# Layer 0 of a four-layer network: PSUM pairs in a ring, both halves of the scores in a row, and the head mixing behind the product with v

## The chip, the cores and the metric

The kernel runs on one core of one Trainium2 chip. The metric is the device time of the whole program in microseconds, the median of several runs. One further execution was taken by the hardware profiler; its trace gives the start and duration of every instruction on each engine.

## The reference

The input is a tensor of 4 images of 512 channels by 32x32 positions. Four layers follow, each of the form x = x + f(gn(x)), where gn is a group normalization over 32 groups. The change touches layer 0 alone, which is an attention with mixed heads:

```python
q = einsum('oc,bct->bot', w_q, xf).reshape(b, heads, hd, t)     # k and v alike; 8 heads of 64, t = 1024
attn = einsum('bhdq,bhdT->bhqT', q, k) * scale
attn = einsum('gh,bhqT->bgqT', w_head, attn)                    # every output head mixes all input heads
attn = softmax(attn, axis=-1)
attn = (attn - mean) / sqrt(var + EPS) * gamma + beta           # one mean and variance per head and image
out = einsum('bhqT,bhdT->bhqd', attn, v)                        # then a projection, a bias, and x is added
```

Layers 1 (a channel gate from a small simulated circuit), 2 (an attention) and 3 (a lookup of eight rows of a memory) follow it.

## The kernel before, in words

Layer 0 treats the images one after another. For one image, q, k and v are projected, and then the 1024 queries are walked in 32 steps of 32 queries (`NS`, `STEPS`), each over all 8 heads and all 1024 keys. All products are in 32-bit floats. The work of a step, in the order in which data passes:

- `scores(b, s, n)` (lines 440 to 465), for the two halves n of the keys: 8 small matmuls of 64 rows (each recorded as two, x16 in the trace) into a pair of PSUM banks, called `sc`, and a copy of the pair by ScalarE into half of the SBUF tile `ss` (L457), of which there are two in turn. Behind the second half, eight DMAs of 128 KB, four issued on SP and four on GpSimd (POOL) in turn, bring the rows of `ss` into the tile `s2` with the heads beside each other (L464). `s2` has two buffers as well.
- `mix(b, s)` (L471), two steps later (`old = s - 2`): 32 small matmuls with the head weights from `s2` into two more pairs of PSUM banks, `mx0` and `mx1`.
- `exps` (L478): ScalarE's exponential of each pair into half of the single tile `e`.
- `turn_keys` (L484): VectorE (DVE) transposes each half of `e` into `eT`, which holds a block of four steps and has two buffers.
- `reduce` (L500): eight `bn_stats` on DVE give the sums and squares of `e`.
- `sums(b, j)` (lines 519 to 570), once for a block of four steps, as a generator that is moved on by `next`: POOL adds up (L532), PE sums over partitions into the bank `pt` (L535), DVE takes the reciprocal out of `pt` (L538), and POOL spreads it by DMA and adds to the sum of squares.
- `apply(b, s - LAG)` (L511): 32 matmuls of `eT` with v into the bank `pv`, `LAG = 6` steps behind the scores. After four of them `take_out` copies `pv` by ScalarE (L574), and `scale` multiplies on POOL and sends the block off.

[...] `pt` serves whatever is small: the projection of v in steps 0 to 6 (`take_v`, L410), the sums (L535), the sum of v in steps 7 and 8 (`sum_v`, L421 and L431), the group means of the next image in steps 25 and 27 (L150 and L160 in `group_coeffs_parts`), those of the previous image's gate from step 28 on, and in steps 12 to 27 of images 1 to 3 the output projection of the image before, a sixteenth in each step (`put_quarter`, L684). The functions `mid` and `piece` hand these out to the steps; `early` issues the loads, on ScalarE's queue, three of 256 KB in each of steps 7 to 10 (what the image before left) and 28 to 31 (the next image and its w_q).

The order is written out by hand. `pin` keeps an instruction behind everything already traced on its engine, so each engine works through its list in the order of the program, and waits at the first entry that is not ready. A tile's buffer is handed on only when the last reader of the old content is done. A step of before is, on PE: scores of half 0, mix of the step two back, scores of half 1, the sums (one step in four), `mid`, the product with v, `piece`. After the 32 steps, `LAG` more run the pipeline dry, with the next image's q projected in the first four; its k follows.

Of the kernel before, what the change touches and what calls it, by code (L numbers as in the profile page):

```python
# [16 lines left out]
P = 128  # L17
# [24 lines left out]
def fast_net(ctx: ExitStack, tc: tile.TileContext, a: dict, out: bass.AP, flag: bass.AP):  # L42
# [6 lines left out]
    stage = ctx.enter_context(ExitStack())  # L49
    ps_a = stage.enter_context(tc.tile_pool(name="ps_a", bufs=1, space=PSUM))  # L50

    pairs = {at: ps_a.tile([P, 2, NB], F32, tag=at, name=at) for at in ("sc", "mx0", "mx1")}
    pv_bank = ps_a.tile([P, NB], F32, tag="pv", name="pv")
    pt_bank = ps_a.tile([P, NB], F32, tag="pt", name="pt")

# [124 lines left out]

    def place(at, name):

        return pairs[at] if at else ps_s.tile([P, 2, NB], F32, tag="sc", name=name)

    def flat2(ps):
        return ps.rearrange("p n q -> p (n q)")

    def tokens(src):
        return lambda k, n: src[:, k, n * NB:(n + 1) * NB]
# [37 lines left out]


    STEPS = T // NS
    LAG = 6  # L230
    NK = T // 4
    apool = ctx.enter_context(tc.tile_pool(name="attn", bufs=1))
    img = [dict() for _ in range(B)]
# [51 lines left out]
    def put_q(q, m):  # L285
        return lambda ps: pin(nc.scalar.copy(q[:, m, :], ps))

    def first():

        I = img[0]  # L290
        xn = I["xn"] = big("xn", "xn_0")
        w = I["w_q"] = eight_k([P, KC, C], "w_q0_0", 0)
        for k in range(KC):
            nc.sync.dma_start(out=xn[:, k, :], in_=x_v[0, :, k, :])
            nc.sync.dma_start(out=w[:, k, :], in_=a["w_q"][:, k, :])
        I["w_k"] = load_w("w_k", "w_k0_0", 1)
# [12 lines left out]

        def means(k):  # L310
            next(parts[k])
            next(parts[k])

        def deviations(k):
            next(parts[k])
            found[k] = next(parts[k])

        def normalize(k):
            gm, rstd, dm = found[k]
            pin(nc.vector.tensor_scalar(  # L320
                xn[:, k, :], xn[:, k, :], gm, rstd, ALU.subtract, ALU.mult))
            pin(nc.gpsimd.tensor_mul(ybar[:, k:k + 1], dm, rstd))

        def multiply(k, m):
            for n in range(T // NB):
                pin(nc.tensor.matmul(
                    pairs[f"mx{m}"][:, n, :],
                    w[:, k, m * P:(m + 1) * P], xn[:, k, n * NB:(n + 1) * NB],
                    start=(k == 0), stop=(k == KC - 1),
                ))  # L330

        stats(0)
        means(0)
        stats(1)
        deviations(0)
        means(1)
        normalize(0)
        for k in range(KC):
            if k + 2 < KC:
                stats(k + 2)  # L340
            multiply(k, 0)
            if k + 1 < KC:
                deviations(k + 1)
            multiply(k, 1)
            if k + 1 < KC:
                normalize(k + 1)
            if k + 2 < KC:
                means(k + 2)
        for m in range(2):
            put_q(q, m)(flat2(pairs[f"mx{m}"]))  # L350
        for m, at in ((2, "sc"), (3, "mx0")):
            project(w, tokens(xn), m, at, put_q(q, m))

    def prepare(b):

# [84 lines left out]
    def scores(b, s, n):  # L440


        I = img[b]
        q, k_ = I["q"], I["k"]
        if n == 0:
            I["ss", s] = eight_k([P, 2, T], f"ss_{b}_{s}", s % 2)
        ss = I["ss", s]
        sc = pairs["sc"]
        for m in range(KC):
            for r in range(2):  # L450
                pin(nc.tensor.matmul(  # L451
                    sc[m * NS:(m + 1) * NS, r, :],
                    q[r * HD:(r + 1) * HD, m, s * NS:(s + 1) * NS],
                    k_[r * HD:(r + 1) * HD, m, n * NB:(n + 1) * NB],
                    start=True, stop=True,
                ))
        pin(nc.scalar.copy(ss[:, :, n * NB:(n + 1) * NB], sc))  # L457
        if n == 0:
            return
        s2 = I["s2", s] = apool.tile([P, 2, T], F32, tag="s2", bufs=2, name=f"s2_{b}_{s}")  # L460
        del I["ss", s]
        for m in range(KC):
            for r in range(2):
                pin(relays[r].dma_start(  # L464
                    out=s2[r * KC + m::NH], in_=ss[m * NS:(m + 1) * NS, r, :]))

    def mix(b, s):
        s2 = img[b].pop(("s2", s))
        for t in range(4):
            for r in range(4):  # L470
                pin(nc.tensor.matmul(  # L471
                    pairs[f"mx{r // 2}"][t * NS:(t + 1) * NS, r % 2, :].rearrange("p (qq k) -> p qq k", qq=2),
                    wmix[r * NS:(r + 1) * NS], s2[r * NS:(r + 1) * NS, :, t * NK:(t + 1) * NK],
                    start=True, stop=True,
                ))

    def exps(s, half):
        pin(nc.scalar.activation(  # L478
            e[:, half].rearrange("p r qq k -> p (r qq k)"), flat2(pairs[f"mx{half}"]), AF.Exp))

    def turn_keys(s, half):

# [4 lines left out]
            e[:, half].rearrange("p r qq (b x) -> p r qq b x", x=NS),  # L487
        ))

    def reduce(b, s):  # L490

        I = img[b]
        j, i = divmod(s, 4)
        if i == 0:
            I["st", j] = apool.tile([P, 4, 4, 2, 6], F32, tag="st", bufs=2, name=f"st_{b}_{j}")
        st = I["st", j]
        for half in range(2):
            for r in range(2):
                for qq in range(2):
                    pin(nc.vector.bn_stats(st[:, i, 2 * half + r, qq, :], e[:, half, r, qq, :]))  # L500

    def apply(b, s):

# [652 lines left out]

    first()
    circuit()
    for m, at in enumerate(("mx1", "sc", "mx0", "mx1")):
        take_k(0, m, at)  # L1160

    def step(b, s, mid, piece):


        I = img[b]
        old = s - 2
        j, part = divmod(s - LAG, 4)
        tiled = 0 <= j < TC
        if tiled and part == 0:
            I["tail"] = sums(b, j)  # L1170
            next(I["tail"])
        if s == 0:
            take_v(b, 0)
        if s < STEPS:
            scores(b, s, 0)
            early(b, s)
        if 0 <= old < STEPS:
            mix(b, old)
            exps(old, 0)
            turn_keys(old, 0)  # L1180
        elif s < STEPS:
            piece(b, s)
        if s < STEPS:
            scores(b, s, 1)
        if 0 <= old < STEPS:
            exps(old, 1)
        if tiled and part == 0:
            next(I["tail"])
        mid(b, s)
        if tiled:  # L1190
            apply(b, s - LAG)
            if part == 3:
                take_out(b, j)
        if 0 <= old < STEPS:
            turn_keys(old, 1)
            reduce(b, old)
        if old >= 0:
            piece(b, s)
        if tiled and part < 3:
            next(I["tail"], None)  # L1200
        if tiled and part < 2 and j > 0:
            next(I["scale"])
        if tiled and part == 3:
            I["scale"] = scale(b, j)
            next(I["scale"])
# [44 lines left out]
    for b in range(B):  # L1250
# [9 lines left out]
            nxt[keys[2]] = load_w(keys[2], f"{keys[2]}_n{b}", 1)  # L1260
        qs = chunks(take_q2, 0) if last else chunks(take_q, b + 1)
        ks = chunks(take_k2, 0) if last else chunks(take_k, b + 1)
        places = dict(zip(range(STEPS, STEPS + KC), ("sc", "sc", "mx0", "mx1")))
        for s in range(STEPS, STEPS + LAG):
            step(b, s, lambda b, s: next(state["behind"], None),
                 lambda b, s: qs[s - STEPS](places[s]) if s in places else None)
# [5 lines left out]
        for m, at in enumerate(("sc", "mx0", "mx1", "mx0")):  # L1272
            ks[m](at)
        if last:
            run_out(instance_norm(b))
            bv2 = apool.tile([P, C], F32, tag="o2", name="bv2")
            nc.sync.dma_start(out=bv2, in_=a["bv"].partition_broadcast(P))
            for i, at in enumerate(("mx0", "mx1", "sc", "mx0")):
                take_v2(0, i, at)
            for m, at in enumerate(("mx1", "sc", "mx0", "mx1")):  # L1280
                put_out(b, m, at)

    stage.close()
    pairs.clear()
# [796 lines left out]
```

## Time and profile before

| | us |
|---|---|
| median of 3 runs (2708.62 to 2716.2) | 2716.14 |
| the profiled execution's own time | 2713.05 |
| its span, first to last instruction | 2711.3 |
| PE busy, 95% of the span | 2578.0 |
| DVE busy, 55% | 1502.3 |
| POOL busy, 46% | 1236.3 |
| ScalarE (ACT) busy, 37% | 1007.6 |
| mean granted TensorE clock | 0.986 |

The first scores of layer 0 start at 75.1 us of the span and the last mixing at 1244.8; layer 0 is thus a little less than half of the program. In a row of a group of instructions stand the line, the engine, the operation, what it writes and reads, how often it ran, its busy time, the mean of one, and how long the engine stood idle just before it and for what. In a row of the timeline stand the start, the duration, the engine, the line and, in brackets, the idle time before it with its releaser.

### The profile page before, as it was taken

The page shows a single profiled execution, that of the slowest core. Times are in us where ns is not written, and L with a number is a line of the kernel's source. Part 1 is how long each engine was busy: PE and PEld are TensorE (multiplying, and loading weights), DVE is VectorE, ACT ScalarE, POOL GpSimd, SP SyncE. Part 2 cuts the span into 40 slices and gives each one's busy share as a digit, 9 for nine tenths or more (in the row PEclk, how much of TensorE's full clock was granted, in tenths as well). Part 3 has the DMA queues.
Part 4 walks back from the last instruction along what each step waited for, and adds up shares of the span by engine and source line. Part 5 has one row for each costly group of instructions (what it writes and reads, how often), then busy time and mean ns, then how long its engine had stood idle before and what let it go on. Part 6 is the DMA issues. An engine that isn't in the chain of part 4 may idle for free.

```text
span 2711.3 us, 46987 instructions
## 1 busy us (share of the span) xinstructions
PE 2578.0 (95%) x18286; PEld 1144.8 (42%) x18286; DVE 1502.3 (55%) x2386; ACT 1007.6 (37%) x1149; POOL 1236.3 (46%) x1891
## 2 busy tenths in 40 slices
PE   8988999989989899989999999999999999999995
PEld 3343534545345443545433443343344334444442
DVE  4487337871478516873146225414513437888887
ACT  1465336551565415652145025215403632121211
POOL 2266415552356514654057027305602725666665
PEclk9999999999999999999999999999999999999997
DMA  2487438880588627885410030022002016767665
GB/s 79 122 209 205 137 92 217 217 226 30 142 227 217 175 61 188 206 201 180 142 55 1 32 124 1 16 78 63 1 31 93 1 51 190 221 187 215 183 183 161
DMA packets 159320, 349.81 MB, mean 129 GB/s; under 512 B 32361, under 2 KB 65129, under 8 KB 155378
## 3 DMA queue, kind: packets, MB, share of 16 engines
q1 hardware_dynamic: 88352, 167.17, 21.5%
q0 software_dynamic: 49152, 142.79, 19.6%
q10 hardware_dynamic: 21586, 36.76, 4.7%
q8 instruction: 147, 2.41, 0.4%
q14 instruction: 83, 0.68, 0.1%
HBM read 178.57 MB, written 33.69 MB: 78 GB/s over the span
## 4 chain that ended last, share of the span: by engine, by line
PE 83%; DMA 6%; ACT 4%; DVE 3%; issue 2%; POOL 2%; SPq 1%; ACTq 0%; POOLq 0%; DVEq 0%
PE at L1094 16%; PE sc_c L973 8%; PE pv_c L1006 8%; PE mx L197 7%; PE sc L451 7%; PE pv L511 6%; DMA s<-ss 5%; PE p L197 4%; PE sc L197 4%; PE pt L410 4%; PE q L197 3%; PE v L209 3%; PE k L197 3%; PE pt L684 3%; ACT ss L457 3%; PE mx L471 2%
## 5 line engine op out<-in xcount | busy, mean ns | idle before, releaser
L484 DVE STREAM_TRANSPOSE eT<-e 128x1024 f32<-128x1024 f32 x256 | 317.4, 1242 | 269.5 <-ACT e L478 267.4
L464 POOL DMA_DIRECT2D s<-ss x512 | 259.3, 514 | 374.1 <-ACT ss L457 306.9
L1111 POOL DMA_INDIRECT got<-in_mem,ix x256 | 280.0, 1094 | 216.1 <-DVE tmx L1117 92.7
L457 ACT COPY ss<-sc 128x1024 f32<-128x1024 f32 x256 | 258.9, 1011 | 259.7 <-PE sc L451 201.5
L967 ACT ACTIVATE eT<-sc_c 128x1024 f32<-128x1024 f32 x256 | 247.8, 1022 | 278.5 <-PE sc_c L973 215.2
L500 DVE BATCH_NORM_STATS2 st<-e 128x6 f32<-128x256 f32 x1024 | 341.5, 405 | 0.0
L991 POOL TENSOR_TENSOR e<-eT 128x1024 f32<-128x1024 f32 x96 | 230.5, 2403 | 176.7 <-ACT eT L967 145.9
L451 PE MATMUL sc<-k,q 64*32 64x512 f32 x4096 | 285.3, 613 | 21.1 <-ACT ss L457 16.2
L478 ACT ACTIVATE e<-mx 128x1024 f32<-128x1024 f32 x256 | 262.5, 1029 | 62.2 <-PE mx L471 31.6
L992 DVE TENSOR_TENSOR eT<-eT,e 128x1024 f32<-128x1024 f32 x96 | 131.5, 1370 | 249.0 <-POOL e L991 248.8
L511 PE MATMUL pv<-eT,v 128*64 128x128 f32 x4096 | 254.8, 278 | 0.0
L511 PEld LDWEIGHTS pv<-eT,v 128*64 128x64 f32 x4096 | 224.5, 138 | 61.6 <-issue 60.0
L973 PE MATMUL sc_c<-q,k 64*128 64x512 f32 x1024 | 238.6, 605 | 2.3 <-DVE xr L650 2.3
L987 POOL TENSOR_TENSOR eT<-eT 128x1024 f32<-128x1024 f32 x32 | 81.1, 2534 | 348.5 <-ACT eT L967 336.9
L1006 PE MATMUL pv_c<-eT,v 128*64 128x512 f32 x1024 | 232.2, 596 | 0.0
L471 PE MATMUL mx<-s,wmix 32*32 32x512 f32 x4096 | 158.9, 621 | 48.3 <-DMA s<-ss 45.3
L1135 DVE SCALAR_TENSOR_TENSOR acc<-got,et,acc 128x512 f32<-128x512 f32 x224 | 168.5, 752 | 8.0
L1033 DVE RECIPROCAL ri_c<-ri_c 128x512 f32<-128x512 f32 x32 | 107.1, 3345 | 96.1 <-ACT ri_c L1032 96.1
L973 PEld LDWEIGHTS sc_c<-q,k 64*128 64x128 f32 x1024 | 94.2, 187 | 131.9 <-issue 73.6
L1099 ACT COPY att<-at 128x1024 f32<-128x1024 f32 x64 | 64.8, 1012 | 218.0 <-PE at L1094 217.9
L587 POOL TENSOR_TENSOR o<-pv,rb 64x256 f32<-64x256 f32 x128 | 111.0, 867 | 68.2 <-ACT pv L574 61.3
L1006 PEld LDWEIGHTS pv_c<-eT,v 128*64 128x64 f32 x1024 | 70.6, 137 | 152.6 <-issue 151.7
(316 smaller groups left out, 3236.0 us busy)
## 6 DMA issues: line engine op xcount, KB each, us to landing
s<-ss SPq DMA_DIRECT2D x512, 128.0 KB
s<-ss POOLq DMA_DIRECT2D x512, 128.0 KB, 4.5
rb<-r POOLq DMA_DIRECT2D x64, 128.0 KB, 6.1
o<-o SPq DMA_DIRECT2D x32, 256.0 KB
xr<-in_x ACTq DMA_DIRECT2D x32, 256.0 KB
x<-xr SPq DMA_DIRECT2D x32, 256.0 KB
xr_c<-x SPq DMA_DIRECT2D x32, 256.0 KB
x<-xr_c SPq DMA_DIRECT2D x32, 256.0 KB
```

What stands on the lines that cost most here:

```text
L197: pin(nc.tensor.matmul(ps[:, n, :], w[:, k, m * P:(m + 1) * P], rhs(k, n), start=(k == 0), stop=(k == KC - 1),))
L451: pin(nc.tensor.matmul(sc[m * NS:(m + 1) * NS, r, :], q[r * HD:(r + 1) * HD, m, s * NS:(s + 1) * NS], k_[r * HD:(r + 1) * HD, m, n * NB:(n ...
L457: pin(nc.scalar.copy(ss[:, :, n * NB:(n + 1) * NB], sc))
L464: pin(relays[r].dma_start(out=s2[r * KC + m::NH], in_=ss[m * NS:(m + 1) * NS, r, :]))
L478: pin(nc.scalar.activation(e[:, half].rearrange("p r qq k -> p (r qq k)"), flat2(pairs[f"mx{half}"]), AF.Exp))
L484: pin(nc.vector.transpose(eT[:, j % 2].rearrange("p b (qq i r) x -> p i r qq b x", qq=2, i=4)[:, i, 2 * half:2 * half + 2], e[:, half].rea ...
L500: pin(nc.vector.bn_stats(st[:, i, 2 * half + r, qq, :], e[:, half, r, qq, :]))
L511: pin(nc.tensor.matmul(pv[r * HD:(r + 1) * HD, gp, :], I["v"][:, t, g * HD:(g + 1) * HD], eT[:, j % 2, t, :, 4 * g:4 * g + 4], start=(t == ...
L973: pin(nc.tensor.matmul(sc[:, r, :], I["k"][r * HD:(r + 1) * HD, m, t * P:(t + 1) * P], I["q"][r * HD:(r + 1) * HD, m, n * NB:(n + 1) * NB] ...
L1006: pin(nc.tensor.matmul(pv[r * HD:(r + 1) * HD, :], I["v"][:, t, h * HD:(h + 1) * HD], e[:, r, :], start=(t == 0), stop=(t == TC - 1),))
L1094: pin(nc.tensor.matmul(sc[:, n * NB:(n + 1) * NB], xn3[b][:, k, tt * P:(tt + 1) * P], memT[k][:, i0:i0 + NB], start=(k == 0), stop=(k == K ...
L1111: pin(nc.gpsimd.indirect_dma_start(out=got[:, i, :], out_offset=None, in_=a["mem"], in_offset=bass.IndirectOffsetOnAxis(ap=ix[:, i:i + 1], ...
```

## The change

The three pairs lose their fixed roles and become a ring. In step s the scores' half n goes to pair (s + n) mod 3, the mixing's halves to pairs (s + 2) mod 3 and s mod 3. Both halves of the scores now stand in a row. The product with v moves ahead of the mixing, which stands behind it together with both exponentials; on DVE the statistics of a half follow the transpose of that half. `LAG` becomes 7, while the sums keep their step (`SUM = 6`) for POOL's part and have PE's part one step later. In a step that has a product with v, `mid` stands ahead of it and `piece` behind the mixing; in the other steps, `piece` stands ahead of the mixing and `mid` behind the first transpose. The projections take their places in the ring. Nothing that is computed changes, and the number of buffers of `s2`, `ss` and `e` stays.

```diff
-    pairs = {at: ps_a.tile([P, 2, NB], F32, tag=at, name=at) for at in ("sc", "mx0", "mx1")}
+    pairs = [ps_a.tile([P, 2, NB], F32, tag=f"pair{i}", name=f"pair{i}") for i in range(3)]
...
-    LAG = 6
+    MIX = 2
+    SUM = 6
+    LAG = 7
...
-        sc = pairs["sc"]
+        sc = pairs[(s + n) % 3]
...
+    def mixed(s, half):
+        return pairs[(s + MIX + 2 + half) % 3]
...
-    def reduce(b, s):
+    def reduce(b, s, half):
...
-        old = s - 2
+        old = s - MIX
+        mixing = 0 <= old < STEPS
+        js, at = divmod(s - SUM, 4)
+        summing = 0 <= js < TC
         j, part = divmod(s - LAG, 4)
         tiled = 0 <= j < TC
-        if tiled and part == 0:
-            I["tail"] = sums(b, j)
+        if summing and at == 0:
+            I["tail"] = sums(b, js)
             next(I["tail"])
         if s == 0:
             take_v(b, 0)
         if s < STEPS:
             scores(b, s, 0)
             early(b, s)
-        if 0 <= old < STEPS:
+            scores(b, s, 1)
+        if summing and at == 1:
+            next(I["tail"])
+        if tiled:
+            mid(b, s)
+            apply(b, s - LAG)
+        else:
+            piece(b, s)
+        if mixing:
             mix(b, old)
             exps(old, 0)
+            exps(old, 1)
             turn_keys(old, 0)
-        elif s < STEPS:
+        if tiled and part == 3:
+            take_out(b, j)
+        if tiled:
             piece(b, s)
-        if s < STEPS:
-            scores(b, s, 1)
-        if 0 <= old < STEPS:
-            exps(old, 1)
-        if tiled and part == 0:
-            next(I["tail"])
-        mid(b, s)
-        if tiled:
-            apply(b, s - LAG)
-            if part == 3:
-                take_out(b, j)
-        if 0 <= old < STEPS:
+        else:
+            mid(b, s)
+        if mixing:
+            reduce(b, old, 0)
             turn_keys(old, 1)
-            reduce(b, old)
-        if old >= 0:
-            piece(b, s)
-        if tiled and part < 3:
+            reduce(b, old, 1)
+        if summing and at > 0:
             next(I["tail"], None)
```

More of the change, by code (lines that the diff above doesn't have):

```diff
@@ L181, in place @@
     def place(at, name):
-        return pairs[at] if at else ps_s.tile([P, 2, NB], F32, tag="sc", name=name)
+        return pairs[at % 3] if at is not None else ps_s.tile([P, 2, NB], F32, tag="sc", name=name)
     def flat2(ps):
@@ L326, in multiply @@
                 pin(nc.tensor.matmul(
-                    pairs[f"mx{m}"][:, n, :],
+                    pairs[m][:, n, :],
                     w[:, k, m * P:(m + 1) * P], xn[:, k, n * NB:(n + 1) * NB],
@@ L349, in first @@
         for m in range(2):
-            put_q(q, m)(flat2(pairs[f"mx{m}"]))
-        for m, at in ((2, "sc"), (3, "mx0")):
-            project(w, tokens(xn), m, at, put_q(q, m))
+            put_q(q, m)(flat2(pairs[m]))
+        for m in (2, 3):
+            project(w, tokens(xn), m, m, put_q(q, m))
     def prepare(b):
@@ L471, in mix @@
                 pin(nc.tensor.matmul(
-                    pairs[f"mx{r // 2}"][t * NS:(t + 1) * NS, r % 2, :].rearrange("p (qq k) -> p qq k", qq=2),
+                    mixed(s, r // 2)[t * NS:(t + 1) * NS, r % 2, :].rearrange("p (qq k) -> p qq k", qq=2),
                     wmix[r * NS:(r + 1) * NS], s2[r * NS:(r + 1) * NS, :, t * NK:(t + 1) * NK],
@@ L478, in exps @@
         pin(nc.scalar.activation(
-            e[:, half].rearrange("p r qq k -> p (r qq k)"), flat2(pairs[f"mx{half}"]), AF.Exp))
+            e[:, half].rearrange("p r qq k -> p (r qq k)"), flat2(mixed(s, half)), AF.Exp))
     def turn_keys(s, half):
@@ L488, in turn_keys @@
         ))
-    def reduce(b, s):
+    def reduce(b, s, half):
         I = img[b]
         j, i = divmod(s, 4)
-        if i == 0:
+        if i == 0 and half == 0:
             I["st", j] = apool.tile([P, 4, 4, 2, 6], F32, tag="st", bufs=2, name=f"st_{b}_{j}")
         st = I["st", j]
[L497 to L500, printed above, removed]
+        for r in range(2):
+            for qq in range(2):
+                pin(nc.vector.bn_stats(st[:, i, 2 * half + r, qq, :], e[:, half, r, qq, :]))
     def apply(b, s):
@@ L1158, in fast_net @@
     circuit()
-    for m, at in enumerate(("mx1", "sc", "mx0", "mx1")):
-        take_k(0, m, at)
+    for m in range(KC):
+        take_k(0, m, m + 1)
     def step(b, s, mid, piece):
         I = img[b]
-        old = s - 2
+        old = s - MIX
+        mixing = 0 <= old < STEPS
+        js, at = divmod(s - SUM, 4)
+        summing = 0 <= js < TC
         j, part = divmod(s - LAG, 4)
         tiled = 0 <= j < TC
-        if tiled and part == 0:
-            I["tail"] = sums(b, j)
+        if summing and at == 0:
+            I["tail"] = sums(b, js)
             next(I["tail"])
@@ L1262, in fast_net @@
         ks = chunks(take_k2, 0) if last else chunks(take_k, b + 1)
-        places = dict(zip(range(STEPS, STEPS + KC), ("sc", "sc", "mx0", "mx1")))
         for s in range(STEPS, STEPS + LAG):
             step(b, s, lambda b, s: next(state["behind"], None),
-                 lambda b, s: qs[s - STEPS](places[s]) if s in places else None)
+                 lambda b, s: qs[s - STEPS](s + 1) if s < STEPS + KC else None)
             if s == STEPS + KC and not last:
@@ L1271, in fast_net @@
             run_out(collect(b, True))
-        for m, at in enumerate(("sc", "mx0", "mx1", "mx0")):
-            ks[m](at)
+        for m in range(KC):
+            ks[m](m + 1)
         if last:
@@ L1277, in fast_net @@
             nc.sync.dma_start(out=bv2, in_=a["bv"].partition_broadcast(P))
[L1278 to L1281, printed above, removed]
+            for i in range(TC // 2):
+                take_v2(0, i, i + 2)
+            for m in range(KC):
+                put_out(b, m, m)
     stage.close()
```

## The prediction

> **What bounds the kernel now.** I read first the busy times, then stretches of layer 0, who waited for whom on PE, and the steps themselves in the timeline. From the page and from the view of busy times by stretch (us, then busy us of PE, weight loads, DVE, ACT, POOL, then granted clock, DMA share, GB/s):
>
> ```profile
> PE 2578.0 (95%) x18286; PEld 1144.8 (42%) x18286; DVE 1502.3 (55%) x2386; ACT 1007.6 (37%) x1149; POOL 1236.3 (46%) x1891
> ...
> 150.00:202.00 52.00, 45.16 (x826) 21.91 (x826) 46.91 (x95) 34.08 (x36) 37.00 (x81) 1.00 0.84 217
> 434.00:456.00 22.00, 16.98 (x292) 7.40 (x290) 17.24 (x33) 17.49 (x22) 13.43 (x27) 0.92 0.94 258
> 456.00:570.00 114.00, 111.39 (x1610) 61.21 (x1606) 96.03 (x198) 64.17 (x67) 67.28 (x148) 1.00 0.81 209
> 570.00:612.00 42.00, 30.83 (x455) 15.86 (x448) 28.52 (x63) 22.50 (x23) 24.76 (x64) 0.88 0.91 246
> ```
>
> PE carries layer 0 where a step has a piece (456 to 570: 98% busy). In image 0 past step 9 (150 to 202) DVE is as full as PE, and in steps 7 to 10 and 28 to 31 of an image the transfers are (shares 0.94 and 0.91). PE's waits from 70 to 1345 us (total, times, longest):
>
> ```profile
> PE mx L471 <- DMA s<-ss: 45.3, 15, 6.7
> PE sc L451 <- ACT ss L457: 16.2, 19, 1.2
> PE pt L535 <- POOL sums L532: 10.4, 10, 2.2
> PE pt L410 <- DVE ial L623: 3.3, 3, 1.1
> PE pt L160 <- DVE ri L538: 2.4, 3, 1.0
> PE pt L841 <- DVE ri L538: 2.4, 3, 1.5
> ```
>
> So no more than some 85 us, 3% of the span, can be gained by order alone. One step (6, image 0) in the timelines of PE and of DVE:
>
> ```profile
> 116.72 1.09 PE L451 MATMUL sc<-k,q 64*32 64x512 f32 x16
> 117.74 1.20 PE L471 MATMUL mx<-s,wmix 32*32 32x512 f32 x32
> 118.98 1.09 PE L451 MATMUL sc<-k,q 64*32 64x512 f32 x16
> 120.00 0.41 PE L535 MATMUL pt<-sums,same 128*128 128x32 f32 x2
> 120.34 1.97 PE L511 MATMUL pv<-eT,v 128*64 128x128 f32 x32
> 122.24 3.70 PE L410 MATMUL pt<-w_v,xn 128*128 128x512 f32 x8
> ```
> ```profile
> 120.14 1.25 DVE L484 STREAM_TRANSPOSE eT<-e 128x1024 f32<-128x1024 f32 x1 [1.07 <-ACT e L478]
> 121.31 0.32 DVE L538 RECIPROCAL ri<-pt 128x32 f32<-128x32 f32 x1
> 122.15 1.25 DVE L484 STREAM_TRANSPOSE eT<-e 128x1024 f32<-128x1024 f32 x1 [0.52 <-ACT e L478]
> 123.32 2.67 DVE L500 BATCH_NORM_STATS2 st<-e 128x6 f32<-128x256 f32 x8
> ```
>
> From start to start PE spends 1.02 on half the scores, 1.13 on the mixing (1.24 with a wait of 0.11 for the copy of half 0), 0.34 on the sums, 1.90 on the product with v, 3.63 on a slice of v; a sixteenth of the projection takes 1.92. DVE needs 1.17 for a transpose and 2.67 for the statistics. The reciprocal stands early in DVE's list, behind one transpose. How tightly it ties PE shows where `mid` writes `pt` right behind the sums (step 30, image 1):
>
> ```profile
> 591.05 0.63 PE L535 MATMUL pt<-sums,same 128*128 128x32 f32 x2
> 591.72 0.36 DVE L538 RECIPROCAL ri<-pt 128x32 f32<-128x32 f32 x1
> 592.13 0.39 PE L160 MATMUL pt<-gsq_b,gavg 128*128 128x4 f32 x2 [0.45 <-DVE ri L538]
> ```
>
> [...] 0.92 over the 22 us from 434 is 3.5 us at half clock, behind a wait of 2.09.
>
> **The change, part by part.**
>
> *Steps 1 and 2 of an image.* Start to start they take 6.91 now, since half 0 waits for the copy of half 1. In the ring both halves and the slice of v fit: 2 x 1.02 + 3.63 = 5.67. 8 x 1.24 = **-9.9**.
>
> *The sums.* POOL's part is a whole step ahead of PE's: its 10.4 go, **-10.4**.
>
> *Half 1 of the scores.* It loses the 0.11 in the 48 steps with a projection piece, -5.3. Where the mixing ends PE's list (steps 3 to 6, and all steps from 8 on without a piece; 16 + 24 + 24 = 64), half 1 of the next step needs the pair of the first mixing half, whose exponential ends 0.15 + 1.02 + 0.05 = 1.22 after the mixing; PE is there 0.95 after it. That is 0.27 in place of 0.11, +10.2. Together **+4.9**.
>
> *`pt` elsewhere.* L160 of the gate (step 30) and L841 no longer meet the sums, -4.8; the L410 wait falls from 3.3 to about 1. **-7**.
>
> *The reciprocal, moved behind a whole step of DVE work.* PE's part of the sums now stands at 2.04 of the steps 7, 11, ... 35, and the reciprocal behind the previous step's second statistics. In step 6 the mixing ends PE's list; from its end DVE needs 0.15 + 1.03 (exponential), 1.17 + 1.33 + 1.17 + 1.33: done 6.3 into step 7, reciprocal at 6.65. In step 7 `mid` issues the sum of v (L421) into `pt`, ready at 2.4; PE stands until 6.7. Behind it in PE's list are the product with v and the mixing, and so ACT and DVE. 4 x 4.3 = +17. In step 27 it is L160: after a step with a piece DVE is done 1.92 earlier and has an addition of 0.47 more, so 2.9 in three images, 4.3 in image 0: +13. **+30**. In steps 15, 19 and 23 the projection piece reaches `pt` at 5.4, the reciprocal ends at 5.2 to 5.9: 9 x 0.5 = **+4.5**.
>
> *The clock.* These eight stops are 3 to 4 us each, as long as those that half-clock windows follow now. [...] Some stops of today go; I count four more windows net, **+7** (0 to +14).
>
> *The transfers of `s2`.* The mixing moves from 1.02 to 3.94 in a step, a deadline 2.9 later. But `s2` has two buffers, and the eight transfers of step s now wait for the mixing in the same step, which ends at 5.15; today they start at the second copy's end, 4.4. On POOL's and SP's queues everything later waits too, `x1` stores among it (hidden: a step of slack). Net 2.2 later. And the copy of half 0 two steps on overwrites `ss`, which those transfers read; it comes behind both exponentials, 2.2 into the step instead of 1.1, so this second deadline gains 0.35, and about 1 before PE sees it. The four waits of image 0's steps 13 to 25 (2.2, 1.5, 2.3, 1.4) go: **-7**. The other 38 us lie in steps 8 to 12 and 28 to 33, where twelve loads of 256 KB stand beside 1.05 MB a step: from step 28, (3.1 + 4.2) MB at 246 GB/s are 30 us against 4 x 5.1 of PE work, and the projection of q waits for w_q, the last of them. The waiting changes place: 0 (bounds -24 and +10).
>
> *LAG 7.* One product with v (1.9) passes from the steps to the drain, where PE never stands: 0. `take_out` behind the exponentials: POOL and the next product have a step: 0; were that gone, 0.6 in a block.
>
> Sum: -9.9 - 10.4 + 4.9 - 7 + 30 + 4.5 + 7 - 7 = **+12**. Against the profiled execution, 2713.05 (its span and 1.75 around it), 2725; the median shown lies 3.1 above it, so **2728**.
>
> **The rivals.** *Faster: the later mixing gives its 2.2 us in full.* The eleven other waits on transfers shrink by 2.2 each, -24, and the sum is -12: 2704. It decides from about 1.1 a wait. For it: the waits end on single late transfers. Against: the DMA share of 0.91 to 0.94 there leaves nothing to catch up with. *No difference: the stops at `pt` are a third shorter,* since PE, held by something else in the step before, lets DVE catch up: +20 and +4 of clock, sum -1, 2715. For it: DVE is no fuller than PE in most stretches. Against: step 6 has no wait on PE today (6.92). *Much slower: ACT becomes the loop in steps without a piece.* Both copies of the scores stand behind both exponentials, and these wait for the single `e`, with DVE at 5.4 a step (2 x 1.17 + 2.67, 0.4 for the rest) against PE's 5.3. At 0.4 in each of the 48 such steps with a product, +19: 2747. Against: ACT has 4 x 1.02 = 4.1 in them.
>
> **How the numbers follow.** Forecast 0.45 (own range 2719 to 2737), faster 0.20, no difference 0.17, much slower 0.18. About 0.3%, 8 us, is what a measurement can tell. Slower by more: 0.38 of the forecast's 0.45, 0.18, 0.02: 0.58. Within: 0.07 + 0.02 + 0.13 = 0.22. Faster: 0.20. The range 2700 to 2748 leaves out the far half of the faster and of the much slower case, 0.18.
>
> **What would show it.** The waits of L451 in steps 1 and 2 and of L535 on L532 gone; L421 and L160 waiting for L538, four times each, near 4 and 3 us; steps 1 and 2 at 5.7, step 7 over 13, steps with a piece at 7.0; L471 waiting less for DMA, and more for the copies L457. It is wrong if L421 starts without a stop in step 7 (the reciprocal is then early), or if steps 28 to 33 together shrink by more than 3 us.

## The result, and the profile after

The kernel after takes 2764.8 us (median of four runs, 2761.5 to 2773.2) against 2716.2 for the kernel before: a ratio of 1.0177, 95% interval 1.0159 to 1.0195, slower by 48.6 us. The profiled execution has a span of 2759.8 us (before 2711.3). All of the loss lies in layer 0: the first scores of layer 2 start at 1418.0 us instead of 1366.7, and what follows takes 1341.8 instead of 1344.7. From 70 us to the first scores of layer 2, PE's waits sum to 121.6 us instead of 86.8, and PE is busy for 1224.0 us instead of 1204.3. The second number grows because more work runs at half clock. In both traces the granted TensorE clock is recorded as 1.0 or 0.5 from 70 us to the first scores of layer 2, and each stretch at 0.5 lasts 3.41 us or two or three times that (6.83, 10.24). A length of 3.41 us is counted as one half-clock window below. That a window in which PE is busy throughout costs half its length, 1.71 us, is an estimate from these two numbers.

The page's busy line, and the view of busy times by stretch, for the stretches of the kernel after that do the same steps as those shown of before (length, busy us of PE, weight loads, DVE, ACT and POOL, then granted clock, DMA share, GB/s):

```profile
PE 2596.1 (94%) x18286; PEld 1158.8 (42%) x18286; DVE 1483.1 (54%) x2387; ACT 994.5 (36%) x1148; POOL 1236.3 (45%) x1891
```
```profile
150.00:202.00 52.00, 49.38 (x864) 22.22 (x862) 47.13 (x96) 36.41 (x39) 36.81 (x82) 1.00 0.90 230
449.00:471.00 22.00, 15.09 (x258) 5.63 (x226) 12.92 (x28) 14.83 (x18) 10.30 (x24) 0.92 0.92 235
476.00:597.00 121.00, 108.94 (x1571) 61.99 (x1570) 91.49 (x192) 59.02 (x64) 62.70 (x140) 0.96 0.77 193
598.00:640.00 42.00, 33.16 (x470) 16.03 (x461) 31.03 (x69) 22.62 (x24) 27.47 (x67) 0.96 0.94 249
```

Steps 13 to 27 of image 1 now last 121.6 us instead of 110.7, from first scores to first scores. In the kernel before PE was 98% busy in about this stretch, at full clock; now it is 90% busy, at a clock of 0.96. Who PE waits for, from 70 to 1400 us (total, times, longest):

```profile
PE pair L477 <- DMA s<-ss: 36.1, 15, 5.2
PE pair L453 <- ACT e L484: 27.3, 66, 1.9
PE pt L423 <- DVE ri L543: 15.3, 4, 3.8
PE pt L160 <- DVE ri L543: 9.9, 4, 2.5
PE pt L540 <- POOL sums L537: 8.5, 4, 4.0
PE pair L453 <- ACT ss L459: 7.8, 8, 2.1
PE pt L689 <- DVE ri L543: 5.9, 8, 1.0
```

The waits for the copies of the scores have halved (16.2 to 7.8), and those for transfers fell from 45.3 to 36.1. New are 27.3 us for the exponential in 66 places. The waits for the reciprocal `ri` in the rows above are 31 us in 16 places; in the kernel before they were 4.8 in 6.

Step 7 of image 1 in the timelines, PE and then DVE (start, length, and in brackets the idle time ahead and what ended it):

```profile
424.14 0.41 PE L540 MATMUL pt<-sums,same 128*128 128x32 f32 x2
428.38 6.52 PE L423 MATMUL pt<-w_v_n,ybar 128*1 128x512 f32 x8 [3.83 <-DVE ri L543]
434.83 1.97 PE L516 MATMUL pv<-eT,v 128*64 128x128 f32 x32
```
```profile
425.55 1.23 DVE L490 STREAM_TRANSPOSE eT<-e 128x1024 f32<-128x1024 f32 x1
426.70 1.36 DVE L505 BATCH_NORM_STATS2 st<-e 128x6 f32<-128x256 f32 x4
427.98 0.34 DVE L543 RECIPROCAL ri<-pt 128x32 f32<-128x32 f32 x1
```

The reciprocal stands behind a whole step's DVE work. PE waits 3.83 us, and then the sum of v takes 6.52 us, because it runs at half clock (0.50 from 428 to 434 us); undisturbed it takes 3.59 (e5 and e10 below). Step 7 lasts 14.4 to 16.0 us in the four images instead of 8.7.

Step 26 is a loss that the prediction did not have: 10.9 to 13.5 us instead of 8.0 to 8.4. POOL's timeline in image 1, and PE's:

```profile
558.12 0.29 POOL L550 TENSOR_SCALAR ok<-ri 128x32 f32<-128x32 f32 x1
569.87 0.20 POOL L155 TENSOR_TENSOR dm_a<-mv_a,gm_a 128x4 f32<-128x4 f32 x1 [11.46 <-DVE gm_a L135]
...
572.44 2.07 POOL L466 DMA_DIRECT2D s<-ss  x4
```
```profile
578.73 3.05 PE L477 MATMUL pair<-s,wmix 32*32 32x512 f32 x32 [3.12 <-DMA s<-ss]
...
588.12 0.41 PE L540 MATMUL pt<-sums,same 128*128 128x32 f32 x2 [1.19 <-POOL sums L537]
591.00 0.39 PE L160 MATMUL pt<-gsq_a,gavg 128*128 128x4 f32 x2 [2.47 <-DVE ri L543]
```

`L155` belongs to the group means of the next image. It isn't pinned, so the scheduler chooses its place, and here it put it ahead of step 24's `s2` transfers in POOL's list; in the kernel before it stood behind them. POOL idles there for 11.46 us, until DVE, itself late, has copied `gm_a`. The POOL half of the transfers is issued at 572.44, the mixing of step 26 waits for it, and the sums and the matmul of the group means (`L160`) stand next. Step 27 takes 12.4 to 15.0 us instead of 6.4 to 7.4. Summed over the four images, steps 7, 26 and 27 lose 26, 17 and 26 us, more than the 51 us by which layer 2 starts later; all the rest of the layer gains some 18.

### The profile page after: what moved, and what is told of

It reads as the page before. It is cut to its first block, busy times and chain, and to the rows that moved or that the text cites. A ratio compares the mean times of both kernels' runs of the same rounds, so it can differ in the third digit from the quotient of the medians.

```text
span 2759.8 us, 47087 instructions
## 1 busy us (share of the span) xinstructions
PE 2596.1 (94%) x18286; PEld 1158.8 (42%) x18286; DVE 1483.1 (54%) x2387; ACT 994.5 (36%) x1148; POOL 1236.3 (45%) x1891
## 4 chain that ended last, share of the span: by engine, by line
PE 79%; DMA 8%; DVE 6%; ACT 3%; issue 2%; POOL 1%; SPq 1%; ACTq 0%; POOLq 0%; DVEq 0%
PE at L1099 16%; PE pair L197 11%; PE sc_c L978 8%; PE pv_c L1011 8%; PE pv L516 5%; DMA s<-ss 5%; PE pt L412 4%; PE p L197 4%; PE pair L477 4%; PE pair L453 3%; PE k L197 3%; PE v L209 3%; PE q L197 3%; DVE st L505 2%; DVE eT L490 2%; ACT e L484 2%
## 5 line engine op out<-in xcount | busy, mean ns | idle before, releaser
L505 DVE BATCH_NORM_STATS2 st<-e 128x6 f32<-128x256 f32 x1024 | 349.9, 403 | 7.0 <-POOL sqs L569 7.0
L484 ACT ACTIVATE e<-pair 128x1024 f32<-128x1024 f32 x256 | 250.4, 1022 | 266.2 <-PE pair L477 196.8
L453 PE MATMUL pair<-k,q 64*32 64x512 f32 x4096 | 273.7, 608 | 35.1 <-ACT e L484 27.3
L459 ACT COPY ss<-pair 128x1024 f32<-128x1024 f32 x256 | 249.6, 1021 | 142.3 <-DMA s<-ss 75.3
L516 PE MATMUL pv<-eT,v 128*64 128x128 f32 x4096 | 260.7, 282 | 0.2 <-ACT pv L579 0.2
L516 PEld LDWEIGHTS pv<-eT,v 128*64 128x64 f32 x4096 | 230.3, 141 | 59.9 <-issue 57.8
L477 PE MATMUL pair<-s,wmix 32*32 32x512 f32 x4096 | 171.1, 631 | 42.3 <-DMA s<-ss 36.1
L453 PEld LDWEIGHTS pair<-k,q 64*32 64x32 f32 x4096 | 56.4, 106 | 218.0 <-ACT e L484 105.0
```

The costliest lines, as they stand in the source:

```text
L453: pin(nc.tensor.matmul(sc[m * NS:(m + 1) * NS, r, :], q[r * HD:(r + 1) * HD, m, s * NS:(s + 1) * NS], k_[r * HD:(r + 1) * HD, m, n * NB:(n ...
L477: pin(nc.tensor.matmul(mixed(s, r // 2)[t * NS:(t + 1) * NS, r % 2, :].rearrange("p (qq k) -> p qq k", qq=2), wmix[r * NS:(r + 1) * NS], s ...
L484: pin(nc.scalar.activation(e[:, half].rearrange("p r qq k -> p (r qq k)"), flat2(mixed(s, half)), AF.Exp))
L516: pin(nc.tensor.matmul(pv[r * HD:(r + 1) * HD, gp, :], I["v"][:, t, g * HD:(g + 1) * HD], eT[:, j % 2, t, :, 4 * g:4 * g + 4], start=(t == ...
```

## The experiments

All but e14 start from the kernel after. The ratios are to the kernel before, run on the same chip. The last columns are from each kernel's trace: when the first scores of layer 2 start, and how many half-clock windows lie wholly ahead of that. These are of one execution each. The mean granted clock of the kernel before ranged from 0.979 to 0.986 over 39 executions, which is some eleven windows at the estimated 1.71 us, so a difference of a few windows says little. The difference between the two kernels is larger than that: by the mean clock of all executions (0.983 and 0.975), the kernel after has some fourteen windows more.

| run | median us | ratio, 95% interval | layer 2 starts | half-clock windows |
|---|---|---|---|---|
| kernel before | 2716.2 | 1 | 1366.7 | 14 |
| kernel after | 2764.8 | 1.0177 (1.0159-1.0195) | 1418.0 | 29 |
| e1 sums late | 2730.4 | 1.0049 (1.0031-1.0067) | 1383.2 | 17 |
| e2 POOL pinned, layers 0 and 2 | 2767.1 | 1.0170 (1.0148-1.0192) | 1407.3 | 28 |
| e3 = e1 + e2 | 2760.5 | 1.0168 (1.0139-1.0198) | 1395.8 | 20 |
| e5 mixing first | 2697.3 | 0.9921 (0.9905-0.9938) | 1351.6 | 17 |
| e6 mixing in the middle | 2717.9 | 1.0005 (0.9989-1.0021) | 1376.9 | 25 |
| e7 POOL pinned, layer 0 | 2752.5 | 1.0144 (1.0115-1.0172) | 1405.9 | 29 |
| e8 mixing late with a piece only | 2722.5 | 1.0019 (1.0008-1.0031) | 1379.9 | 26 |
| e9 = e5 with LAG 6 | 2714.5 | 0.9993 (0.9979-1.0007) | 1367.5 | 15 |
| e10 stops filled | 2756.6 | 1.0140 (1.0113-1.0167) | 1415.3 | 22 |
| e11 half the statistics | 2742.6 | 1.0100 (1.0073-1.0128) | 1395.7 | 26 |
| e12 LAG 6 | 2814.9 | 1.0352 (1.0330-1.0373) | 1470.7 | 35 |
| e13 = e5, mixing by halves | 2688.0 | 0.9897 (0.9879-0.9916) | 1344.7 | 19 |
| e14 kernel before, LAG 7 | 2747.3 | 1.0118 (1.0087-1.0150) | 1402.4 | 19 |
| e15 mixing by halves | 2759.9 | 1.0164 (1.0125-1.0202) | 1412.5 | 35 |
| e16 = e13 + e7 | 2699.2 | 0.9933 (0.9909-0.9957) | 1343.8 | 17 |

**e1: the sums behind the piece.**

```diff
-        if summing and at == 1:
-            next(I["tail"])
         if tiled:
             mid(b, s)
 ...
+        if summing and at == 1:
+            next(I["tail"])
         if mixing:
             reduce(b, old, 0)
```

> The kernel after, with PE's part of the sums and the reciprocal moved within the same step, from ahead of the product with v to behind the piece: on DVE the reciprocal then stands in front of the statistics and not behind those of the step before, and `pt` is next written a step later. Theory (the late reciprocal holds `pt`): the waits of `pt` for `ri` (15.3 of L423, 9.9 of L160, 5.9 of L689) fall below 5 us together, step 7 falls from about 15 to about 9 us, and half-clock windows go with the stops, some 7 of them at 1.7: 2764.8 - 27 - 12 = about 2726. Step 26 stays at 11 to 13 us, since POOL's order is untouched. Rival (the transfers of s2 set the time, the stops only cover their lateness): the waits of L477 for DMA grow by nearly what the others lose, and the time stays above 2752.

2730.4. The waits for `ri` of `L423`, `L160` and `L689` are gone (1.7 us are left in the second part of the sum of v), step 7 is 9.2 us in every image, and twelve half-clock windows went. The edit takes 34 us off. Not all of it is the reciprocal, though: step 26, expected to stay at 11 to 13 us, fell to 5.3 to 8.0. With nothing pinned, `L155` now stands behind step 24's transfers. From POOL's timeline in image 1:

```profile
544.57 2.08 POOL L466 DMA_DIRECT2D s<-ss  x4 [0.90 <-issue]
...
551.39 0.20 POOL L155 TENSOR_TENSOR dm_a<-mv_a,gm_a 128x4 f32<-128x4 f32 x1 [2.96 <-DVE gm_a L135]
```

Step 7, in which POOL's order has no part, became 24 us shorter over the four images, and step 26 22 us; the run doesn't separate the two causes further. DVE's lateness also shows elsewhere now: PE's part of the sums waits for the projection's addition `L655` (18.8 us in 12 places), and the gate's `L841` in the drain for `ri` (9.3 us, 0.8 in the kernel after).

**e2, e7 and e3: POOL's order.** In e2 the group-mean operations keep the program's order in layer 0, and also in the images of layer 2; in e7 in layer 0 alone; e3 is e1 and e2 together.

```diff
-        hold = pin if n == 1 else lambda ins: ins
+        hold = pin if n == 1 or tag[0] in "ac" else lambda ins: ins
```

and in e7:

```diff
-        hold = pin if n == 1 else lambda ins: ins
+        hold = pin if n == 1 or tag in ("a1", "a2", "a3", "c0") else lambda ins: ins
```

> The kernel after, with POOL's group-mean operations of layer 0 (L155 to L157, L124) held in the order in which the program writes them, behind the step's issue of the s2 transfers; in the kernel after they stand up to two steps further ahead on POOL, in front of them. All other engines keep their order. Theory (POOL, stopped at L155, issues a step's s2 transfers late): step 26 falls from 11-13.5 us to about 8, the stop of L453 and L477 behind it goes, and with it part of step 27's half clock: 4 x 4.3 + 4 x 1.7 = 24, about 2741. Rival (the transfers of steps 24 to 26 are late because s2 has two buffers and the mixing comes last in a step): POOL waits instead for the mixing, and the time stays within 5 us of 2764.8.

> The kernel after, with POOL's group-mean operations held in program order for the four calls inside layer 0 alone; the run e2_pool_pin held those of layer 2's images too, where it lost 16 us. Theory (POOL's order costs what the first scores of layer 2 gained there, 1418.0 - 1407.3 = 10.7): 2754. Rival (POOL's order is no cause, the difference of the two profiles was chance): 2761 to 2768.

> Both edits together: the sums behind the piece, and POOL's group-mean operations held behind the s2 transfers. Theory (two separate causes, with the half-clock windows that follow each): the gains add, 39 + 24 = 63, about 2702, below the 2716.2 of the kernel before; granted clock back at 0.986 or above. Rival (the rest of the change, a later mixing and seven steps of lag, costs something too): it stays above 2725.

e2 shortened step 26 to 5.3, 7.9 and 7.3 us in images 0 to 2, and layer 2 started 10.7 us earlier; but layer 2 then took 1358.2 us instead of 1341.8. It held layer 2's own group means too, and 13.7 us at half clock stand there, at 1485, 1724 and 1966 us, that the kernel after doesn't have. With layer 0 alone (e7) the median is 12 us lower and layer 2 starts 12 us earlier, as the second expectation had it, though the intervals of the two ratios just overlap. In image 3 step 26 still takes 11.8 us in e7: there another operation that isn't pinned, `L913`, stands ahead of step 24's transfers and holds POOL for 10.05 us. So POOL's order is a part of the loss, a smaller one than the 24 us first put to it. In e3 the gains do not add. Layer 2 pays its 15 us again, and layer 0 ends 12.6 us later than in e1. In e1 `L155` had already moved behind the transfers, so the pin had nothing left to gain there, and it delays the group means (`L160` waits 6.0 us for POOL's `gsq_a`, and the drains of images 1 and 2 are 9 and 6 us longer).

**e5: the mixing first.** One part of the change undone, the place of the mixing:

```diff
+        if mixing:
+            mix(b, old)
+            exps(old, 0)
+            exps(old, 1)
         if tiled:
             mid(b, s)
             apply(b, s - LAG)
         else:
             piece(b, s)
         if mixing:
-            mix(b, old)
-            exps(old, 0)
-            exps(old, 1)
             turn_keys(old, 0)
```

> The kernel after, with the mixing and the exponentials moved back ahead of the small work and the product with v (still behind both halves of the scores). Theory (the late reciprocal and POOL's order make the loss, the place of the mixing does not): the waits of `pt` for `ri` stay at 25 to 35 us; L453's wait for the exponential (27.3) goes, as the product and the piece now lie between, and L477 waits for the copy of half 0 instead, some 0.15 x 100 = 15: 2750 to 2765. Rival (the place of the mixing makes the loss, as it frees s2 later and puts the copies behind both exponentials): s2 is free 2 us earlier, L477's wait for DMA falls from 36 below 25, and the time falls below 2740.

2697.3, 67 us less than the kernel after and 0.8% faster than the kernel before. The theory had put this at 2750 or more and kept the waits for `ri`; it fell. Waits from 70 to 1400 us, and step 7 of image 1 on PE:

```profile
PE pair L477 <- DMA s<-ss: 35.0, 10, 6.3
...
PE pt L540 <- POOL sums L537: 5.2, 4, 2.2
...
PE pt L160 <- DVE ri L543: 1.3, 4, 0.4
```
```profile
401.44 0.41 PE L540 MATMUL pt<-sums,same 128*128 128x32 f32 x2
401.77 1.18 PE L477 MATMUL pair<-s,wmix 32*32 32x512 f32 x32
402.89 3.59 PE L423 MATMUL pt<-w_v_n,ybar 128*1 128x512 f32 x8
```

`L423` starts without a stop: the reciprocal, at 402.10 in DVE's timeline, is now early enough, although its place in DVE's list is that of the kernel after. The 27.3 us for the exponential are gone too. The rival was right on the time, but not by its reason: the wait for the transfers is as large as before (35.0 against 36.1). The price of the early mixing is seen in the steps with a piece, 7.15 us against 6.77: the 32 matmuls of the mixing now take 1.52 there, not 1.14. From the waits of the two kernels: 31 for `ri`, 27 for the exponential, 7 for the copies, 3 for POOL's sums and, for twelve windows, up to 21 (12 x 1.71), less 48 x 0.38 = 18, is 71, against 66 us between the two starts of layer 2. That is an estimate; all of PE's waits up to layer 2 fell by 62 us (121.6 to 59.9). POOL's order also changed in e5: `L155` stands behind step 24's transfers, as in the kernel before, in e1 and in e6. So the 67 us are the place of the mixing together with what the scheduler makes of it; no run holds POOL's order fixed while the mixing moves.

**e6: the mixing in the middle,** behind the small work of `mid`, ahead of the product:

```diff
         if tiled:
             mid(b, s)
+        if mixing:
+            mix(b, old)
+            exps(old, 0)
+            exps(old, 1)
+        if tiled:
             apply(b, s - LAG)
...
```

> The kernel after, with the mixing and the exponentials moved ahead of the product with v (of the slice of v in steps 0 to 6), but left behind the small work of `mid`. Theory (the later the mixing stands in a step, the later DVE's 6.3 us of exponential, transposes and statistics end, and the waits are what of it sticks out): the product's 1.9 us off each wait, so L423 waits 0.6 instead of 3.8 in step 7, L160 0.6 instead of 2.5 in step 27, and L453's 27.3 for the exponential go: 2764.8 - 27 - 13 - 8 - some 12 of half-clock windows = about 2705. Rival (what matters is only that the mixing stood ahead of `mid`, between the sums and the next write to `pt`): the waits of L423 and L160 stay above 2 us each, and the time above 2735.

2717.9. The loss goes with the place: 2697 ahead of everything, 2718 behind the small work, 2765 behind the product. The waits for `ri` are 2.6 (`L423`) and 5.9 (`L160`), those for the exponential at the scores are gone. The size of the last gap was missed, as 25 half-clock windows stayed: in step 27 of image 1 PE stands 1.77 us for POOL's part of the sums and 1.53 for `ri` ahead of the mixing, its half-clock product takes 3.30 instead of 1.97, and step 27 lasts 12 to 13 us in the four images against 8.3 to 9.0 in e5.

**e8: late only where a piece follows.**

```diff
+        full = b > 0 and OUT <= s < OUT + 16
+        if summing and at == 1 and not full:
+            next(I["tail"])
+        if mixing and not full:
+            mix(b, old)
...
             apply(b, s - LAG)
...
-        if mixing:
+        if summing and at == 1 and full:
+            next(I["tail"])
+        if mixing and full:
             mix(b, old)
...
```

> A new order: in the 48 steps with a projection piece the mixing stands behind the product with v (as in the kernel after, with the sums between them), in all others ahead of it (as in e5_mix_first). Theory (in a step with a piece the piece itself hides the exponential, and the product hides the copy of half 0; only steps that end with the mixing lose): 0.38 less in each of 48 steps, less some 4 for the sums behind L166 in step 27: 2697.3 - 18 + 4 = 2683. Rival (DVE is late behind a late mixing in any step): waits of L453 for the exponential and steps of 8.2 come back, and the time is 2700 or above.

2722.5; the rival. Undisturbed steps with a piece took 6.77, as hoped, but `L689` waited for `ri` in 8 places (5.6 us), steps of 8.2 us came back, and step 26 took 10.8 to 13.4 us in images 1 to 3, against 7.15 in e5, which is 15 us of the 25 between the two runs. In these images `L155` stands ahead of step 24's transfers again and holds POOL for 10 to 11.5 us. A piece behind the mixing does not repair it: what comes late is not PE's next matmul but DVE's results a step later.

**e11: less work on DVE.**

```diff
-                pin(nc.vector.bn_stats(st[:, i, 2 * half + r, qq, :], e[:, half, r, qq, :]))
+                pin(nc.vector.bn_stats(st[:, i, 2 * half + r, qq, :], e[:, half, r, qq, 0:NK // 2]))
```

> The kernel after, with the statistics of the scores taken from half of the elements (128 in place of 256 of each group), so that DVE has some 1.3 us less to do in each step; the order of every engine is kept. It leaves out half of what the sums are computed from, and its result differs. Theory (DVE's chain ends too late behind the late mixing): L423's wait falls from 3.8 to 2.5 each, L160's and L689's by 1 or to nothing, L453's waits for the exponential (27.3, of which a third are those in which `e` was held by DVE) to about 18: 2764.8 - 5 - 4 - 5 - 9 and 8 of half-clock windows = 2734. Rival (ACT, not DVE, is late: both copies behind both exponentials): L453 keeps 24 us or more of its wait, and the time stays above 2750.

2742.6, 22 us less. From its waits:

```profile
PE pair L453 <- ACT e L484: 27.1, 66, 1.9
...
PE pt L423 <- DVE ri L543: 11.0, 4, 2.8
```

The four statistics took 0.83 us instead of 1.36, so 1.06 us a step, and `L423` waits 1.1 less each time, `L160` 1.1 less, `L689` not at all: those waits measure how late DVE is. The wait for the exponential did not move, so DVE's load doesn't set that one, and in this part the theory was wrong.

**e15: the exponential's own wait.** The matmuls of half 0 go first:

```diff
-        for t in range(4):
-            for r in range(4):
+        for half in range(2):
+            for t in range(4):
+                for r in (2 * half, 2 * half + 1):
...
```

> The kernel after with the mixing's matmuls ordered by half, so that half 0 is complete, and its exponential can start, some 0.5 us earlier. Theory (L453's 27.3 us come from the exponential of half 0 behind a mixing that ends a step, not from DVE): the wait of 0.3 to 0.4 in some 60 steps goes, 27.3 falls below 12, and 2764.8 - 16 = 2749. Rival (the exponential waits for DVE to free `e`, or for the copies ahead of it on ACT): the wait stays above 20 us and the time within 6 of 2764.8.

```profile
PE pair L453 <- ACT e L485: 11.1, 10, 1.5
```

The wait fell from 27.3 us in 66 places to 11.1 in 10, as the theory had it, but the time stayed (2759.9, interval overlapping that of the kernel after), as the rival had it. Light steps became 0.10 shorter (5.24), windows at half clock rose from 29 to 35, and step 7 was as long as before. PE's waits up to layer 2 fell by 20 us (121.6 to 101.1), so what was saved isn't waited elsewhere; but PE was busy 10 us longer (1224.0 to 1234.5), in line with the six windows more. Why they came, and whether they come in every execution, the run does not show.

**e10: more work in the stops.**

```diff
+        if s in (TC - 1, NEXT - 1):
+            for _ in range(4 if s < TC else 2):
+                pin(nc.tensor.matmul(
+                    pv_bank, gavg, I["q"][:, 0, 0:NB], start=True, stop=True))
         if tiled:
             mid(b, s)
```

> The kernel after with more work: four matmuls of 0.91 us (128x512, into `pv` before its block begins, never read) ahead of `mid` in step 7 and two in step 27, where PE stands for the reciprocal. They put off nothing that could have run in a wait of 3.8 and 2.5 us. Theory (part of the loss is the half-clock window that follows a stop): step 7 falls from 14.4-16.0 to about 12.6 us, eight fewer half-clock windows at most, 4 x 2.5 + 4 x 1 = 14 less: 2751, though PE has 20 us more work. Rival (the stops alone count, the windows are of no weight or follow other stops): 2763 to 2772.

With some 20 us more matmul work the kernel took 2756.6, 8 us less; the two intervals just overlap. Step 7 in PE's timeline:

```profile
422.79 3.68 PE L1190 MATMUL pv<-q,gavg 128*128 128x512 f32 x8
426.78 3.59 PE L423 MATMUL pt<-w_v_n,ybar 128*1 128x512 f32 x8 [0.31 <-DVE ri L543]
```

The sum of v starts no earlier than in the kernel after (it is 6.6 us into the step there as well) but runs at full clock, 3.59 against 6.52 us. Step 7 lasts 13.1 us in all four images, together 8 us less than in the kernel after; the half-clock windows at 127, 428, 759 and 1090 us have gone. How long a stop must be for half clock to follow, the runs do not show. In the kernel before, it followed all seven stops of 3.49 to 6.67 us, and also those of 1.50, 2.09 and 2.18 (ahead of 1256.00, 438.63 and 248.97), but not one of 2.30 (ahead of 214.71; clock 1.00 from 211 to 222). In the kernel after, stops of 3.19 and 3.04 us (ahead of 616.72 and 910.13) left the clock at 1.00 (613 to 622 and 905 to 916), while the stop of 2.47 us ahead of 591.00, with another of 1.19 before it, was followed by half clock (0.50 from 591.5 to 594.5): the product behind it took 3.61 us instead of 1.97.

**e9 and e12: the lag.** `LAG = 6` in place of 7, in e5 and in the kernel after.

> e5_mix_first with LAG 6 in place of 7: the mixing ahead of the product with v, and the product six steps behind the scores. Theory (the seventh step is needed only because the late mixing makes the transposes late): with the mixing early the last transpose of a block ends 3.0 into the next step, where the product starts at 3.3, so nothing waits: 2697 +- 6. Rival (the seventh step carries part of e5's gain): above 2708.

> The kernel after with LAG 6 in place of 7, the mixing still behind the product with v. Theory (the late mixing makes the last transpose of a block end 4.9 us behind the mixing, so that in step 4j + 6 the product would wait for it): waits of L516 for L490 of 2.4 in light steps and 0.5 behind a step with a piece, some 42 us in all, and half-clock windows behind the longer ones, 20: about 2825. Rival (the lag is of no weight, or the product's wait only takes the place of the waits for `ri`): 2757 to 2773.

With the mixing late, six steps cost 50 us more:

```profile
PE pv L516 <- DVE eT L490: 80.2, 29, 3.8
```

The transposes of a block end when the product is already due, twice the wait that was expected. So the seventh step belongs to the late mixing. But with the mixing early it isn't idle either: e9 lost 17 us against e5, with 8.7 us of the same wait in 13 places (0.4 each in twelve of them, steps 14, 18, 22 and 26 of images 1 to 3, and 3.6 in the last drain) and 5 us more for transfers. The theory's margin, transposes done 0.3 us ahead of the product, was worked out for light steps; in those with a piece DVE also has the addition `L655`, which may be what eats it. Image 0, which has no pieces, has none of these waits.

**e13 and e16: better orders.** e13 is e5 with the mixing of e15, e16 adds the pin of e7.

> e5_mix_first with the mixing's matmuls ordered by half: the sixteen of half 0 first, then those of half 1, which write the pair that the copy of scores' half 0 frees. Theory (the 0.38 us that each mixing lasts longer in e5 than in the kernel after is the wait for that copy): steps with a piece fall from 7.15 to 6.8, and steps 2 to 6 by as much; 0.35 x (48 + 20) = 24 less than 2697.3, about 2673. Rival (DVE, with some 5.2 us a step, or the transfers take the time up again as soon as PE is faster): 2688 or above, with more waits of L477 for DMA or for the exponential.

> e13 (the mixing ahead of the product, by halves) with POOL's group-mean operations of layer 0 held in program order. Theory (with the mixing early DVE is early too, and POOL's order costs only the waits of PE for POOL's part of the sums, 6.1 us): 2688 - 6 = 2682. Rival (holding them delays the coefficients of the next image and lengthens the drain, as in e3_sums_pool): 2688 or above.

e13 at 2688.0 is the fastest, 1.0% ahead of the kernel before, but the gain was 9 us and not 24: steps with a piece fell only from 7.15 to 7.10, so the 0.38 is not simply the wait of half 1 for the copy. What it is was not settled; where the sums stand ahead of the mixing it is gone (1.14 us for the 32 matmuls, against 1.48). e16 is no faster than e13: `L160` again waits for `ri` (6.1 us). In e13 and in e1, to which e16 and e3 add the pin, `L155` stood behind step 24's transfers already; there, holding it gained nothing.

**e14: the lag in the kernel before** (`LAG = 7`, nothing else).

> The kernel before with LAG 7 in place of 6 and nothing else (sums and product a step later). Theory (in the order of the kernel before, DVE is early enough; the seventh step pays only where transposes run late): L511 waits for no transpose before or after, one product of 1.9 us passes to the drain: 2714 to 2722. Rival (the lag itself is the gain that e5 has over e9, 17 us): 2703 or less.

2747.3, which neither had. In that order the transpose of half 0 stands ahead of the product. With seven steps it writes, in steps 4j + 10, what the last quarter of block j's product still has to read: that quarter is computed from a later block's data, and waits for this transpose (34.1 us in 21 places, 1.36 in a step with a piece). The run says nothing of the lag by itself, which stays open, but it shows why the change had to move the transpose behind the product.

## Why the prediction was wrong

The direction was right (slower, given 0.58), but 2728 was 37 us short, and 2764.8 lies outside 2700 to 2748. By its own steps:

- *Steps 1 and 2* (0 and 1 in the count of the other steps): expected 5.67 each, -9.9 in all; measured 5.51, -11.2. Right.
- *The sums:* -10.4 expected, -1.9 measured: 8.5 us of waits are left, four stops of 0.8 to 4 us in step 27. The early place was undone by POOL, late from step 24 on; with POOL's order pinned (e7) these waits are gone.
- *Half 1 of the scores:* light steps 5.34 against 5.18, +0.16 as predicted; undisturbed steps with a piece 6.77 and not 6.99, better by up to 48 x 0.22 = 11. And in e15 most of this wait went without a measurable gain.
- *The reciprocal:* 17, 13 and 4.5 predicted for `L423`, `L160` and `L689`; measured 15.3, 9.9 and 5.9. The mechanism and its sizes were right; in e11, with 1.06 us less for DVE, each of the first two waits falls by 1.1.
- *The clock:* +7, four windows at 1.7 each, the author's estimate. There are fifteen more, up to 15 x 1.71 = 26 us: the largest mis-sized term. Only the eight stops were counted, and as if one window followed each at most and most replaced others; in the kernel after two often follow (at 428, 759 and 1236 us), and covering step 7's stops took six of them away (e10).
- *The transfers:* -7. Right where it named the waits: those in steps 13 to 25 of image 0 fell from 7.4 to 0.5. The waiting from step 29 on did change place: it fell by some 15 us, yet from step 28 to the next scores (of the next image or of layer 2) the four images together take 489 us instead of 487, with a product with v more in each. That all of `L477`'s waits for DMA fell by 9.2, near the 7, is luck, as 14.3 us are new in step 26. These were not foreseen: "on POOL's and SP's queues everything later waits too" looked at what stands behind the transfers. What stands ahead of them, `L155` placed by the scheduler and waiting for a late DVE, is the missing step: some 12 us (e7).
- *LAG 7: 0.* Right in that the product with v waits for transposes in neither kernel. But the term looked only at the product's own place. Without the seventh step the late mixing would cost 50 us more (e12), and with the mixing early it still gives some 17 (e9).

So the steps that failed are the clock term, four windows where there were fifteen, the sums, and the transfers' look at POOL's list. With 19 more for the clock and 12 for POOL's order, in which the sums' 8 are contained, less 11 for the steps with a piece, +12 becomes +32, of 48.6 measured. This is an estimate: the clock's part is an upper bound, smaller differences of the other terms are left out, and the rest is not assigned. Behind these terms stands one thing: the mixing's move was priced by what it does to the transfers and to one reciprocal. It delays some 6 us of exponential, transposes and statistics into the next step, and so everything that reads DVE: `pt`, the group means, POOL's queue, the transposes. e5 and e6 show that the place of the mixing makes the loss, 67 us with all that follows from it; e11 shows that DVE's lateness is one way in which it does.

Of the rivals, *faster* and *no difference* did not happen, although a kernel with all the rest of the change is faster (e5). *ACT becomes the loop* had the nearest time, 2747, for a reason that the runs do not bear out: the waits on ACT were there (27.3 us), and taking most of them away did not change the time measurably (e15).

## What to carry to other kernels

When a producer is moved within a software-pipelined step, follow its whole chain, with its length against the length of a step, and price every reader of what comes out late; where one reader was repaired alone (e1), others waited instead. Count each stop of PE with the half clock recorded behind it (here 3.83 us of stop, and 2.93 more for the matmuls that followed), and look in every in-order queue for work that the scheduler may place ahead of what PE needs (here `L155`, at which POOL idled for 11.46 us). Look there after every edit, too: that place changed in runs whose edit had nothing to do with POOL. A move that needs another (here the lag of seven) to be bearable at all deserves a run without it.

## What was not expected of the hardware

A stop of 3.83 us cost 6.8 us, as the matmuls behind it took 6.52 instead of 3.59 us. With unread matmuls in such stops step 7 was 2 us shorter in an image, and the median 8 us lower with intervals that just overlap, at 20 us more of PE work. And in the kernel after, windows at half clock came in runs of up to three: 10.2 us from 789 us on, behind a wait of 3.48 us for transfers and with a further stop of 0.91 us inside. Whether that stop is itself a result of the half clock, no run shows.
